# Chosen attention heads: LSTM states summed as they come, weights loaded by head number on the sync queue, TensorE's work in program order

## The chip, the cores and the metric

The kernel runs on one core of a Trainium2 chip (trn2). The core has five engines with a queue of instructions each: PE (matrix multiplication and transposes, results in PSUM banks), DVE (vector operations), ACT (scalar functions, also copies), POOL (general-purpose cores, which here also issue indirect DMAs) and SP (which issues DMAs). The metric is the time of the whole kernel on the device, in microseconds; lower is better.

## What is computed

The reference is a network of two layers on x of shape [8, 512, 256] (8 batch rows, 512 positions, width 256), with a condition vector per row. Layer 0 is a modulated linear map, an attention with graph weights, an LSTM and a mixture of attention heads; layer 1 is an adaptive low-rank map, causal attention, a recurrent layer and a mixture of experts. The change concerns the LSTM's output and what reads it, the mixture of heads:

```python
dist = jax.nn.softmax(jnp.mean(x @ Wr + br, axis=1), axis=-1)   # x: the LSTM's states
top_vals, top_idx = jax.lax.top_k(dist, 4)                      # 4 of 16 heads per row
g = ...                                                         # softmax gate of each chosen head
Qk, Kk, Vk = chosen heads of (x @ W + b), times g               # 64 wide each
attn = softmax(Qk @ Kk.T / 8)                                   # [8, 4, 512, 512]
out = (attn @ Vk).reshape(B, S, 256) @ Wo + bo
```

The mean over positions goes before the product with Wr, so the kernel needs the sum of each LSTM state over the 512 positions. Which four heads a batch row uses is known only once all 512 steps of the LSTM are done.

## The kernel before

**Order of work.** The profiled execution shows: layer 0's modulation and attention up to about 600 us; the LSTM, 512 steps of 2.4 us, up to 1896 us; the chosen heads (`routed_heads`) from 1896 to 2353 us; then layer 1.

**LSTM.** Each step multiplies the last state with the weights on PE (L631), transposes the gates on DVE (L637, L641), applies tanh on ACT (L638, L649) and writes the new state, doubled, into `ring` (DVE, L650), a buffer of eight steps. Each eighth step, POOL copies the eight states, halved, into hT, which holds all states as [128, 2, 8, 512] (L662). Side work is laid into the steps: the next projection of the inputs (`proj`, sums at L601), the rest of the attention (`rest`, in steps 0 to 6 of 16) and the first layer-1 weights (`extra`, in steps 13 to 15 of 16, while it lasts; its sum `ws` is DVE's L988). PE, ACT and DVE follow the order in which this loop is written (`manual_schedule`).

**Choosing the heads** (L687 to L754). SP loads wo, wr, br, and later pmv. DVE sums hT over the positions (hsum, L694), PE multiplies with wr (pl), DVE and ACT compute softmax, the four largest and their numbers, gates gq and gh, and from the head numbers two tables of row offsets: wof for the weights, bof for the biases.

**The loads by head** (`gather`, L758). For each batch row b eight indirect DMAs on POOL fetch w, the weights of four heads (L763; each takes 128 rows of 192 numbers, one row per partition, from the offsets in wof), and four fetch the biases bs (L770). w, bs and the reordered copy wq have two buffers each; bg, the biases times the gates, has three. `prepare` makes wq with four copies on POOL (L784) and bg with two operations on DVE (L789, L790).

**The 32 units.** A unit is a batch row b and a chunk c of 128 positions; `scores`, `transposes` and `average` run as a pipeline of three stages, one unit apart:

- `scores(n)`: PE computes four score tiles pe, one per head, each [128, 512] in a PSUM bank of its own (L822, eight matmuls); DVE takes the maximum nm (L828), ACT the exponential with its sum (L829), DVE the reciprocal rc and the scaling sm (L831, L833).
- `transposes(n - 1)`: for each head, PE transposes four 128x128 blocks into pt (L841; two PSUM banks); DVE copies heads 0 and 2, ACT heads 1 and 3 into eT (L843).
- `average(n - 2)`: PE multiplies eT with v into po (L855, heads 0 and 1, then 2 and 3), ACT scales it into oT (L857).

Per batch row once: `project` (pp on PE L800, qk on ACT L802 and L804; queries in the unit c = 1 of the row before, keys in c = 2), `values` (pv L814, copied on DVE L815; in c = 3), `output` (px L863, added to xT on DVE L864), and once in the stage the constants of layer 1 (ppv, L928, at n = 9). pp, pv, po, px and ppv share two PSUM banks (pool pj). Here no order is written out: a planner in the framework orders every engine's instructions, and they wait for one another by semaphores.

Of the kernel before, what the change touches and what calls it, by code (L numbers as in the profile page):

```python
# [551 lines left out]
def lstm(K, hT, rest, weights, extra):  # L552
# [15 lines left out]
    with ExitStack() as es:  # L568
# [54 lines left out]
        for t in range(S):  # L623
            if t % RB == 0:
                last = ring
                ring = rp.tile([P, RB, 2, B], F32, name="ring", tag="ring")
            for dst, lo, hi in parts(t):
                for k in range(2):
                    hp = h0[:, k, :] if t == 0 else (ring[:, t % RB - 1, k] if t % RB else last[:, RB - 1, k])
                    for j in range(4):  # L630
                        mm(dst[32 * j : 32 * j + B], hp, wh[:, k, j * 256 + lo : j * 256 + hi], start=False, stop=(k == 1))  # L631
            if t + 1 < S:
                if t % XB == XB - 1:
                    xw = nxt
                seed(t + 1, xw, parts(t + 1)[:1])
            G = sp.tile([P, 4, 2, 32], F32, name="G", tag="G")
            nc.vector.transpose(G[:, 0:2].rearrange("p g k b -> p (g k b)"), pgi[t % 2].rearrange("p g n -> p (g n)"))  # L637
            nc.scalar.activation(X[:, 0:2], G[:, 0:2, :, 0:B], AF.Tanh)  # L638
            to = sp.tile([P, 2, B], F32, name="to", tag="to")
            for g, ps, th in ((2, pgg, X[:, 2]), (3, pgo, to)):  # L640
                nc.vector.transpose(G[:, g].rearrange("p k b -> p (k b)"), ps)  # L641
                nc.scalar.activation(th, G[:, g, :, 0:B], AF.Tanh)
            pr = sp.tile([P, 2, 2, B], F32, name="pr", tag="pr")
            STT(pr[:, 1], X[:, 1], 1.0, X[:, 3], ALU.add, ALU.mult)
            STT(pr[:, 0], X[:, 0], 1.0, X[:, 2], ALU.add, ALU.mult)
            X = sp.tile([P, 4, 2, B], F32, name="X", tag="X")
            STT(X[:, 3], pr[:, 1], 0.5, pr[:, 0], ALU.mult, ALU.add)
            th = sp.tile([P, 2, B], F32, name="th", tag="th")
            nc.scalar.activation(th, X[:, 3], AF.Tanh, scale=0.5)  # L649
            STT(ring[:, t % RB], to, 1.0, th, ALU.add, ALU.mult)  # L650
            if t % XB == 7 and t - 7 + XB < S:
                proj = project(t - 7 + XB)
                nxt = next(proj)
            next(proj, None)
            if t % XB < 7:
                next(rest, None)
            if t % XB > 12:
                next(extra, None)
            if t + 1 < S:
                seed(t + 1, xw, parts(t + 1)[1:])  # L660
            if t % RB == RB - 1:
                nc.gpsimd.tensor_scalar(  # L662
                    hT[:, :, :, t - RB + 1 : t + 1], ring.rearrange("p t k b -> p k b t"), 0.5, None, ALU.mult
                )
# [2 lines left out]

def routed_heads(K, hT, T):
# [4 lines left out]
    with ExitStack() as es:  # L677
# [13 lines left out]


        hsum = wp.tile([P, 2, B], F32, name="hsum")
        nc.vector.tensor_reduce(hsum, hT, AX.X, ALU.add)  # L694
        pl = pj.tile([B, NH], F32, name="pl", tag="pj")
        for k in range(2):
            mm(pl, hsum[:, k, :], wr[:, k, :], start=(k == 0), stop=(k == 1))
        lg = wp.tile([B, NH], F32, name="lg")
        nc.vector.scalar_tensor_tensor(lg, pl, 1.0 / S, br, ALU.mult, ALU.add)
        nm = wp.tile([B, 1], F32, name="nm")  # L700
        sm = wp.tile([B, 1], F32, name="sm")
        nc.vector.tensor_reduce(nm, lg, AX.X, ALU.max, negate=True)
# [32 lines left out]
            r = slice(64 * f, 64 * f + 64)  # L735
            nc.vector.tensor_copy(gh[r], g4[r, :, :, :, f])

        pcol = wp.tile([P, 2], F32, name="pcol")
        nc.gpsimd.iota(pcol, [[P, 2]], base=0, channel_multiplier=1, allow_small_or_imprecise_dtypes=True)
        pmod = wp.tile([P, 2], F32, name="pmod")  # L740
        for a in range(4):
            r = slice(32 * a, 32 * a + 32)
            nc.vector.tensor_scalar(pmod[r, 0:1], pcol[r, 0:1], -64.0 * (a // 2), None, ALU.add)
            nc.vector.tensor_scalar(pmod[r, 1:2], pcol[r, 0:1], -32.0 * a, None, ALU.add)
        wof = wp.tile([P, B, 2, NA], I32, name="wof")
        for k in range(2):
            nc.vector.tensor_scalar(wof[:, :, k, :], gb[:, :, 1, :], float(D), pcol[:, k : k + 1], ALU.mult, ALU.add)

        bof = wp.tile([P, B, 4], I32, name="bof")
        nc.vector.tensor_scalar(bof[:, :, 0], gs[:, :, 1], 64.0, pmod[:, 1:2], ALU.mult, ALU.add)  # L750
# [7 lines left out]
        def gather(b):  # L758
            w = gp.tile([P, 2, NA, 192], F32, name="w", tag="w")
            bs = gp.tile([P, 4, 3], F32, name="bs", tag="bs")  # L760
            for k in range(2):
                for s in range(NA):
                    nc.gpsimd.indirect_dma_start(  # L763
                        out=w[:, k, s, :],
                        out_offset=None,
                        in_=inp["moh_w"],
                        in_offset=bass.IndirectOffsetOnAxis(ap=wof[:, b, k, s : s + 1], axis=0),
                    )
            for i in range(4):
                nc.gpsimd.indirect_dma_start(  # L770
                    out=bs[:, i, :],
                    out_offset=None,
                    in_=inp["moh_b"],
                    in_offset=bass.IndirectOffsetOnAxis(ap=bof[:, b, i : i + 1], axis=0),
                )
            W[b] = w, bs

        def prepare(b):

            w, bs = W[b]  # L780
            wr_ = gp.tile([P, 2, 2, 2, P], F32, name="wq", tag="wq")
            for k in range(2):
                for i in range(2):
                    nc.gpsimd.tensor_copy(  # L784
                        wr_[:, k, i].rearrange("p h (s r) -> p h s r", s=NA),
                        w[:, k, :, 64 * i : 64 * i + 64].rearrange("p s (h r) -> p h s r", h=2),
                    )
            bg = gp.tile([P, 4], F32, name="bg", tag="bg", bufs=3)
            nc.vector.tensor_scalar(bg[:, 0:2], bs[:, 0:2, 0], gq[:, b : b + 1], None, ALU.mult)  # L789
            nc.vector.tensor_tensor(bg[:, 2:4], bs[:, 2:4, 2], gh[:, b, 0, :], ALU.mult)  # L790
            W[b] = w, bs, wr_, bg

        def project(b, i):
# [3 lines left out]
            for h in range(2):  # L797
# [4 lines left out]
                    nc.scalar.activation(Q[b][:, i, h, :], pp, AF.Identity, bias=bg[:, h : h + 1], scale=gq[:, b : b + 1])  # L802
                else:
                    nc.scalar.activation(Q[b][:, i, h, :], pp, AF.Identity, bias=bs[:, h, 1:2])  # L804

        def values(b):
            w = W[b][0]
            v = V[b] = qp.tile([P, 4, NA, 64], F32, name="v", tag="v")
            for cc in range(2):
                pv = pj.tile([P, 2, NA, 64], F32, name="pv", tag="pj")  # L810
                for c in range(2):
                    at = (2 * cc + c) * P
                    for k in range(2):
                        mm(pv[:, c], hT[:, k, b, at : at + P], w[:, k, :, 128:192], start=(k == 0), stop=(k == 1))  # L814
                nc.vector.tensor_copy(v[:, 2 * cc : 2 * cc + 2], pv)  # L815

        def scores(b, c):
            pe = [psc.tile([P, S], F32, name="pe", tag="pe") for _ in range(NA)]
# [16 lines left out]
        def transposes(b, c):  # L835
            sm = SM.pop((b, c))
            ET[b, c] = []
            for a in range(NA):
# [3 lines left out]
                t = ep.tile([P, 4, P], F32, name="eT", tag="eT")  # L842
                (nc.scalar.copy if a % 2 else nc.vector.tensor_copy)(t, pt)  # L843
                ET[b, c].append(t)

        def average(b, c):
            eT, bg = ET.pop((b, c)), W[b][3]
# [3 lines left out]
            for pr in range(2):  # L851
                for j in range(4):
                    for f in range(2):
                        a = 2 * pr + f
                        mm(po[64 * f : 64 * f + 64, pr, :], V[b][:, j, a, :], eT[a][:, j, :], start=(j == 0), stop=(j == 3))  # L855
            for pr in range(2):
                nc.scalar.activation(OT[b][:, pr, c * P : (c + 1) * P], po[:, pr, :], AF.Identity, bias=bg[:, 2 + pr : 3 + pr], scale=gh[:, b, 0, pr : pr + 1])  # L857

        def output(b):
            for dc in range(2):  # L860
                px = pj.tile([P, S], F32, name="px", tag="pj")
                for pr in range(2):
                    mm(px, wo[:, pr, dc * P : (dc + 1) * P], OT[b][:, pr, :], start=(pr == 0), stop=(pr == 1))  # L863
                nc.vector.scalar_tensor_tensor(xT[:, dc, b, :], px, K.cols[:, 4 + dc : 5 + dc], xT[:, dc, b, :], ALU.add, ALU.add)  # L864

        gather(0)
        prepare(0)
        gather(1)
        project(0, 0)
        project(0, 1)  # L870
        values(0)
        units = [(b, c) for b in range(B) for c in range(4)]
        for n in range(len(units) + 2):
            if n < len(units):
                b, c = units[n]
                scores(b, c)
                if b + 1 < B:
                    if c == 0:
                        prepare(b + 1)
                    elif c == 3:  # L880
                        values(b + 1)
                    else:
                        project(b + 1, c - 1)
                if c == 3 and b + 2 < B:
                    gather(b + 2)
                if n == 9:
                    T.constants(K, wp, pj.tile([64, D], F32, name="ppv", tag="pj"))
            if 0 < n <= len(units):
                transposes(*units[n - 1])
            if n > 1:  # L890
                b, c = units[n - 2]
                average(b, c)
                if c == 3:
                    output(b)

# [804 lines left out]
def two_layers_kernel(tc, *args):  # L1702
    inp, out = dict(zip(NAMES, args)), args[-1]
    with ExitStack() as es:
        K = State(tc, inp, es)
        with tc.tile_pool(name="wd", bufs=1, space=DRAM) as dp, ExitStack() as eh:
# [5 lines left out]
            def states():  # L1712
                hp = eh.enter_context(tc.tile_pool(name="hT", bufs=1, side="right"))
                lw = el.enter_context(tc.tile_pool(name="l_w", bufs=1, side="right"))
                return hp.tile([P, 2, B, S], F32, name="hT"), lw

            with ExitStack() as e0:
# [143 lines left out]
```

## Time and profile before

| what | us |
|---|---|
| median of three runs | 4411.29 (4408.77 to 4412.3) |
| profiled execution | 4559.43 |
| its span, first to last instruction | 4557.5 |
| chosen heads: whole stage | 1896 to 2353, 457 |
| of these before the first projection on PE (L800) | 32.9 |
| PE busy in the stage | 357.6 |
| DVE, ACT, POOL busy in the stage | 225.9, 174.8, 104.1 |

The profiled execution is 3.4% longer than the median. In it PE is busy for 79% of the span and DVE for 50%; the mean clock granted to PE is 0.901 of full speed. The ends of matmuls are modelled in this profile, and a wait for several semaphores is put down to the one that came last. A row of a timeline gives start, duration, engine, line, operation, output and inputs, count, and in brackets the engine's idle time before it and what ended it. L numbers are lines of the kernel before.

### The profile page before, as it was taken

The numbers are of one execution on the slowest core, as the hardware profiler recorded it, in microseconds if no ns is written. First come the engines' busy times: TensorE is split into PE (matmuls) and PEld (weight loads), VectorE is DVE, ScalarE is ACT, GpSimd is POOL, SyncE is SP. The second block draws the span as 40 slices with busy tenths as digits, with TensorE's granted clock in tenths as the row PEclk, the third lists the DMA queues.
The fourth block names the chain that finished last, engine by engine and source line by source line (L and its number), as shares of the span: only waits on it lengthen the run. The fifth ranks groups of instructions, "written<-read, shape, count | busy, mean of one in ns | idle before, by whom it ended". The sixth has DMA issues, their size and how long they took to land.

```text
span 4557.5 us, 148382 instructions
## 1 busy us (share of the span) xinstructions
PE 3581.0 (79%) x63838; PEld 2335.1 (51%) x63838; DVE 2275.6 (50%) x8665; ACT 1421.0 (31%) x5215; POOL 898.2 (20%) x1534
## 2 busy tenths in 40 slices
PE   7800068888888888578889999999999988989785
PEld 5500045555555555345545555555555545667564
DVE  3300046666666666444547676666667633333332
ACT  2100013333333333234434334343334312323142
POOL 0077700000000000142102222222212211020312
PEclk9955579999999999888999999999999988989698
DMA  2100000000000000200000000000000021343267
GB/s 79 38 1 1 0 17 19 14 19 19 14 4 4 4 4 4 65 25 15 8 2 1 1 1 1 1 1 1 1 1 1 1 96 40 112 124 117 92 209 221
DMA packets 104003, 157.22 MB, mean 34 GB/s; under 512 B 21264, under 2 KB 73776, under 8 KB 102960
## 3 DMA queue, kind: packets, MB, share of 16 engines
q1 hardware_dynamic: 72064, 108.46, 7.9%
q0 software_dynamic: 18432, 23.28, 1.8%
q10 hardware_dynamic: 12848, 15.99, 1.0%
q8 instruction: 500, 8.19, 0.8%
q14 instruction: 159, 1.30, 0.1%
HBM read 107.82 MB, written 41.02 MB: 33 GB/s over the span
## 4 chain that ended last, share of the span: by engine, by line
PE 58%; DVE 20%; another core or an unknown queue 8%; issue 5%; ACT 5%; DMA 2%; POOL 0%; ACTq 0%; SPq 0%; DVEq 0%; POOLq 0%
PE pgi L631 7%; PE pg L1279 5%; PE pe L1113 4%; PE po L1167 3%; PE pt L1152 3%; DVE G L641 3%; PE px L597 3%; PE pp L1080 3%; PE pv L1098 3%; PE px L1183 2%; DVE G L637 2%; PE pg L1501 2%; ACT th L649 2%; PE pe L822 2%
## 5 line engine op out<-in xcount | busy, mean ns | idle before, releaser
L631 PE MATMUL pgi<-wh,ring 128*8 128x128 f32 x8176 | 319.3, 274 | 215.8 <-DVE ring L650 211.8
L1133 ACT ACTIVATE sm<-sm,nm 128x388 f32<-128x388 f32 (+3 forms) x512 | 283.6, 555 | 252.4 <-DVE nm L1129 250.9
L1284 DVE STREAM_TRANSPOSE ring<-h 128x64 f32<-128x64 f32 x512 | 125.6, 245 | 446.0 <-ACT h L1283 429.2
L638 ACT ACTIVATE X<-G 128x32 f32<-128x32 f32 x512 | 117.0, 229 | 686.0 <-DVE G L637 677.5
L631 PEld LDWEIGHTS pgi<-wh,ring 128*8 128x8 f32 x8176 | 177.8, 89 | 280.0 <-DVE ring L650 277.6
L441 PE MATMUL pA<-ohl,ohh 128*32 128x16 f32 x512 | 29.9, 215 | 369.7 <-DVE ohl L438 284.6
L637 DVE STREAM_TRANSPOSE G<-pgi 128x128 f32<-128x128 f32 x512 | 162.1, 317 | 271.4 <-PE pgi L631 271.4
L1279 PE MATMUL pg<-wh,ring 128*8 128x64 f32 x8176 | 229.5, 236 | 80.3 <-DVE ring L1284 67.7
L1080 PE MATMUL pp<-hn,wqkv 128*128 128x512 f32 x512 | 281.0, 689 | 11.0 <-DVE hn L1066 11.0
L420 POOL DMA_INDIRECT gath<-sdr,idx x256 | 253.1, 989 | 99.5 <-issue 77.7
L1283 ACT ACTIVATE h<-pg 128x64 f32<-128x64 f32 x512 | 114.2, 223 | 504.1 <-PE pg L1279 439.3
L1113 PE MATMUL pe<-kt,qt 32*128 32x132 f32 (+3 forms) x2048 | 259.2, 472 | 0.1
L1142 POOL COPY pme<-sm 128x4 f32<-128x4 f32 x512 | 126.4, 247 | 655.1 <-DVE sm L1138 650.6
L1152 PE MATMUL pt<-ident,sm 128*128 128x128 f32 x1280 | 211.1, 287 | 45.8 <-DVE eT L1154 45.6
L1152 PEld LDWEIGHTS pt<-ident,sm 128*128 128x128 f32 x1280 | 151.0, 145 | 166.0 <-DVE eT L1154 77.3
L1279 PEld LDWEIGHTS pg<-wh,ring 128*8 128x8 f32 x8176 | 127.1, 93 | 196.2 <-DVE ring L1284 151.8
L1167 PE MATMUL po<-eT,v 128*64 128x128 f32 x2560 | 206.1, 281 | 17.2 <-DVE rr L1084 15.3
L441 PEld LDWEIGHTS pA<-ohl,ohh 128*32 128x32 f32 x512 | 28.4, 156 | 371.9 <-DVE ohl L438 285.9
L631 PE MATMUL pgo<-wh,ring 128*8 128x64 f32 x8176 | 208.7, 219 | 0.1
L611 PE MATMUL pgi<-xw,ident 128*8 128x128 f32 x4096 | 208.0, 273 | 0.8 <-DVE xw L601 0.5
L631 PE MATMUL pgg<-wh,ring 128*8 128x64 f32 x8176 | 208.5, 219 | 0.0
L1138 DVE TENSOR_SCALAR sm<-sm,rc 128x388 f32<-128x388 f32 (+3 forms) x512 | 199.8, 433 | 5.2
(499 smaller groups left out, 7884.0 us busy)
## 6 DMA issues: line engine op xcount, KB each, us to landing
w<-in_experts_dram SPq DMA_DIRECT2D x124, 384.0 KB
x<-xs SPq DMA_DIRECT2D x124, 128.0 KB
ys<-y SPq DMA_DIRECT2D x124, 128.0 KB
xs<-zero ACTq DMA_DIRECT2D x2, 4736.0 KB
w<-in_ada_w_dram SPq DMA_DIRECT2D x16, 512.0 KB
gath<-sdr,idx POOLq DMA_INDIRECT x256
out_dram<-acc SPq DMA_DIRECT2D x32, 128.0 KB
wqkv<-in_w_qkvT_dram SPq DMA_DIRECT2D x1, 3072.0 KB
```

What stands on the lines that cost most here:

```text
L420: nc.gpsimd.indirect_dma_start(out=gath[:, c : c + 1], out_offset=None, in_=sdr[:, :], in_offset=bass.IndirectOffsetOnAxis(ap=idx[:, c : c ...
L597: mm(px[:, n * 512 : n * 512 + 512], xc[:, k], wx[:, k, n * 512 : n * 512 + 512], start=(k == 0), stop=(k == 1))
L611: mm(dst[32 * j : 32 * j + B], pick[:, t % XB, :], xw[:, j * 256 + lo : j * 256 + hi], start=True, stop=False)
L631: mm(dst[32 * j : 32 * j + B], hp, wh[:, k, j * 256 + lo : j * 256 + hi], start=False, stop=(k == 1))
L637: nc.vector.transpose(G[:, 0:2].rearrange("p g k b -> p (g k b)"), pgi[t % 2].rearrange("p g n -> p (g n)"))
L1080: mm(pp, T.wqkv[:, k, 0 : 2048].rearrange("p (i g h n) -> p i g h n", i=2, g=4, h=2)[:, i, g, h], self.hn[b][:, k, :], start=(k == 0), sto ...
L1113: mm(pe[a][:, 0 : w - lo], q[r, h, at], k[r, h, lo:w], start=(h == 0), stop=(h == 1))
L1133: nc.scalar.activation(sm[a][:, 0:w], sm[a][:, 0:w], AF.Exp, bias=nm[:, a : a + 1], scale=-1.0, accum_out=su[:, a : a + 1])
L1138: nc.vector.tensor_scalar(sm[a][:, 0:w], sm[a][:, 0:w], rc[:, a : a + 1], None, ALU.mult)
L1152: nc.tensor.transpose(pt[:, j, :], sm[a][:, 4 + j * P : 4 + (j + 1) * P], K.ident)
L1167: mm(po[64 * f : 64 * f + 64, pr, :], v[:, j, 64 * a : 64 * a + 64], eT[a][:, j, :], start=(j == 0), stop=(j == c))
L1279: mm(pg[32 * j : 32 * j + B], hp, M.wh[:, k, 64 * j : 64 * j + 64], start=False, stop=(k == 1))
```

## The change

Four edits go together.

1. **Sums within the LSTM.** Each eighth step, after the step's other work, DVE sums `ring` over its eight states into `hpart` (64 such partial sums, [128, 64, 2, 8], 4 KB per partition, in the pool that holds hT). hsum then sums hpart instead of hT; since the ring holds doubled states, the factor is 0.5/S instead of 1/S.
2. **Weights by head number on SP.** wof holds the first row of each chosen head. SP reads it from SBUF into a register (`value_load`) and issues one plain DMA per head (256 rows, 192 KB) with that offset: four register loads and four DMAs per batch row in place of eight indirect DMAs on POOL. The four indirect DMAs of the biases stay on POOL. In the built kernel SP's order is: the loads for b = 0 and 1, then all other 24 register loads, then the other DMAs.
3. **wq of b = 0 on DVE**, the others as before on POOL.
4. **PE in program order.** In the loop over the units PE follows the order in which the code is written. project, values, average, output and constants become generators that yield after each piece (half of a projection, of the values, of the average or of the output); `give` runs one piece of the first that has any left. Per unit PE's order is: scores, first half of average, transposes of head 0 and 1, second half of average, transposes of head 2, a piece of project or values, transposes of head 3, the next piece, then what is left (output, constants). DVE and ACT are still ordered by the planner; outside the LSTM's sums and this stage, all engines have the order of before.

```diff
@@ -659,6 +659,7 @@
             if t + 1 < S:
                 seed(t + 1, xw, parts(t + 1)[1:])
             if t % RB == RB - 1:
+                nc.vector.tensor_reduce(K.hpart[:, t // RB], ring.rearrange("p t k b -> p k b t"), AX.X, ALU.add)
                 nc.gpsimd.tensor_scalar(
                     hT[:, :, :, t - RB + 1 : t + 1], ring.rearrange("p t k b -> p k b t"), 0.5, None, ALU.mult
                 )
@@ -667,6 +668,14 @@
 
 
 
+
+
+def give(queue):
+
+    while queue:
+        if next(queue[0], queue) is not queue:
+            return
+        queue.pop(0)
 
 
 def routed_heads(K, hT, T):
@@ -691,12 +700,12 @@
 
 
         hsum = wp.tile([P, 2, B], F32, name="hsum")
-        nc.vector.tensor_reduce(hsum, hT, AX.X, ALU.add)
+        nc.vector.tensor_reduce(hsum, K.hpart.rearrange("p n k b -> p k b n"), AX.X, ALU.add)
         pl = pj.tile([B, NH], F32, name="pl", tag="pj")
         for k in range(2):
             mm(pl, hsum[:, k, :], wr[:, k, :], start=(k == 0), stop=(k == 1))
         lg = wp.tile([B, NH], F32, name="lg")
-        nc.vector.scalar_tensor_tensor(lg, pl, 1.0 / S, br, ALU.mult, ALU.add)
+        nc.vector.scalar_tensor_tensor(lg, pl, 0.5 / S, br, ALU.mult, ALU.add)
         nm = wp.tile([B, 1], F32, name="nm")
         sm = wp.tile([B, 1], F32, name="sm")
         nc.vector.tensor_reduce(nm, lg, AX.X, ALU.max, negate=True)
@@ -735,16 +744,15 @@
             r = slice(64 * f, 64 * f + 64)
             nc.vector.tensor_copy(gh[r], g4[r, :, :, :, f])
 
-        pcol = wp.tile([P, 2], F32, name="pcol")
-        nc.gpsimd.iota(pcol, [[P, 2]], base=0, channel_multiplier=1, allow_small_or_imprecise_dtypes=True)
+        wof = wp.tile([P, B, NA], I32, name="wof")
+        nc.vector.tensor_scalar(wof, gb[:, :, 1, :], float(D), None, ALU.mult)
+        pcol = wp.tile([P, 1], F32, name="pcol")
+        nc.gpsimd.iota(pcol, [[0, 1]], base=0, channel_multiplier=1, allow_small_or_imprecise_dtypes=True)
         pmod = wp.tile([P, 2], F32, name="pmod")
         for a in range(4):
             r = slice(32 * a, 32 * a + 32)
             nc.vector.tensor_scalar(pmod[r, 0:1], pcol[r, 0:1], -64.0 * (a // 2), None, ALU.add)
             nc.vector.tensor_scalar(pmod[r, 1:2], pcol[r, 0:1], -32.0 * a, None, ALU.add)
-        wof = wp.tile([P, B, 2, NA], I32, name="wof")
-        for k in range(2):
-            nc.vector.tensor_scalar(wof[:, :, k, :], gb[:, :, 1, :], float(D), pcol[:, k : k + 1], ALU.mult, ALU.add)
 
         bof = wp.tile([P, B, 4], I32, name="bof")
         nc.vector.tensor_scalar(bof[:, :, 0], gs[:, :, 1], 64.0, pmod[:, 1:2], ALU.mult, ALU.add)
@@ -758,14 +766,9 @@
         def gather(b):
             w = gp.tile([P, 2, NA, 192], F32, name="w", tag="w")
             bs = gp.tile([P, 4, 3], F32, name="bs", tag="bs")
-            for k in range(2):
-                for s in range(NA):
-                    nc.gpsimd.indirect_dma_start(
-                        out=w[:, k, s, :],
-                        out_offset=None,
-                        in_=inp["moh_w"],
-                        in_offset=bass.IndirectOffsetOnAxis(ap=wof[:, b, k, s : s + 1], axis=0),
-                    )
+            for s in range(NA):
+                row = nc.sync.value_load(wof[0:1, b, s : s + 1], min_val=0, max_val=(NH - 1) * D)
+                nc.sync.dma_start(out=w[:, :, s, :], in_=inp["moh_w"][bass.ds(row, D), :].rearrange("(k p) n -> p k n", p=P))
             for i in range(4):
                 nc.gpsimd.indirect_dma_start(
                     out=bs[:, i, :],
@@ -781,7 +784,7 @@
             wr_ = gp.tile([P, 2, 2, 2, P], F32, name="wq", tag="wq")
             for k in range(2):
                 for i in range(2):
-                    nc.gpsimd.tensor_copy(
+                    (nc.gpsimd if b else nc.vector).tensor_copy(
                         wr_[:, k, i].rearrange("p h (s r) -> p h s r", s=NA),
                         w[:, k, :, 64 * i : 64 * i + 64].rearrange("p s (h r) -> p h s r", h=2),
                     )
@@ -802,6 +805,7 @@
                     nc.scalar.activation(Q[b][:, i, h, :], pp, AF.Identity, bias=bg[:, h : h + 1], scale=gq[:, b : b + 1])
                 else:
                     nc.scalar.activation(Q[b][:, i, h, :], pp, AF.Identity, bias=bs[:, h, 1:2])
+                yield
 
         def values(b):
             w = W[b][0]
@@ -813,6 +817,7 @@
                     for k in range(2):
                         mm(pv[:, c], hT[:, k, b, at : at + P], w[:, k, :, 128:192], start=(k == 0), stop=(k == 1))
                 nc.vector.tensor_copy(v[:, 2 * cc : 2 * cc + 2], pv)
+                yield
 
         def scores(b, c):
             pe = [psc.tile([P, S], F32, name="pe", tag="pe") for _ in range(NA)]
@@ -842,6 +847,7 @@
                 t = ep.tile([P, 4, P], F32, name="eT", tag="eT")
                 (nc.scalar.copy if a % 2 else nc.vector.tensor_copy)(t, pt)
                 ET[b, c].append(t)
+                yield
 
         def average(b, c):
             eT, bg = ET.pop((b, c)), W[b][3]
@@ -853,8 +859,11 @@
                     for f in range(2):
                         a = 2 * pr + f
                         mm(po[64 * f : 64 * f + 64, pr, :], V[b][:, j, a, :], eT[a][:, j, :], start=(j == 0), stop=(j == 3))
+                if pr == 0:
+                    yield
             for pr in range(2):
                 nc.scalar.activation(OT[b][:, pr, c * P : (c + 1) * P], po[:, pr, :], AF.Identity, bias=bg[:, 2 + pr : 3 + pr], scale=gh[:, b, 0, pr : pr + 1])
+            yield
 
         def output(b):
             for dc in range(2):
@@ -862,36 +871,44 @@
                 for pr in range(2):
                     mm(px, wo[:, pr, dc * P : (dc + 1) * P], OT[b][:, pr, :], start=(pr == 0), stop=(pr == 1))
                 nc.vector.scalar_tensor_tensor(xT[:, dc, b, :], px, K.cols[:, 4 + dc : 5 + dc], xT[:, dc, b, :], ALU.add, ALU.add)
+                yield
+
+        def constants():
+            T.constants(K, wp, pj.tile([64, D], F32, name="ppv", tag="pj"))
+            yield
 
         gather(0)
         prepare(0)
         gather(1)
-        project(0, 0)
-        project(0, 1)
-        values(0)
+        for pieces in (project(0, 0), project(0, 1), values(0)):
+            for _ in pieces:
+                pass
         units = [(b, c) for b in range(B) for c in range(4)]
-        for n in range(len(units) + 2):
-            if n < len(units):
-                b, c = units[n]
-                scores(b, c)
-                if b + 1 < B:
-                    if c == 0:
-                        prepare(b + 1)
-                    elif c == 3:
-                        values(b + 1)
-                    else:
-                        project(b + 1, c - 1)
-                if c == 3 and b + 2 < B:
-                    gather(b + 2)
-                if n == 9:
-                    T.constants(K, wp, pj.tile([64, D], F32, name="ppv", tag="pj"))
-            if 0 < n <= len(units):
-                transposes(*units[n - 1])
-            if n > 1:
-                b, c = units[n - 2]
-                average(b, c)
-                if c == 3:
-                    output(b)
+
+
+        with K.tc.manual_schedule(engines={mybir.EngineType.PE}):
+            for n in range(len(units) + 2):
+                more = [average(*units[n - 2])] if n > 1 else []
+                if n < len(units):
+                    b, c = units[n]
+                    scores(b, c)
+                    if b + 1 < B:
+                        if c == 0:
+                            prepare(b + 1)
+                        else:
+                            more.append(values(b + 1) if c == 3 else project(b + 1, c - 1))
+                    if c == 3 and b + 2 < B:
+                        gather(b + 2)
+                    if n == 9:
+                        more.append(constants())
+                if n > 1 and units[n - 2][1] == 3:
+                    more.append(output(units[n - 2][0]))
+                give(more)
+                for a, _ in enumerate(transposes(*units[n - 1]) if 0 < n <= len(units) else ()):
+                    if a:
+                        give(more)
+                while more:
+                    give(more)
 
 
 
@@ -1712,6 +1729,7 @@
             def states():
                 hp = eh.enter_context(tc.tile_pool(name="hT", bufs=1, side="right"))
                 lw = el.enter_context(tc.tile_pool(name="l_w", bufs=1, side="right"))
+                K.hpart = hp.tile([P, S // 8, 2, B], F32, name="hpart")
                 return hp.tile([P, 2, B, S], F32, name="hT"), lw
 
             with ExitStack() as e0:
```

## The prediction

> **What bounds the kernel now.** I read the page's slices first, then the stage's stretches, then the engines' timelines at three places. The page (slices of 113.9 us) shows the routed-heads stage, 1896 to 2353 us, in slices 17 to 21:
>
> ```profile
> PE   7800068888888888578889999999999988989785
> POOL 0077700000000000142102222222212211020312
> PEclk9955579999999999888999999999999988989698
> ```
>
> PE rises to 8 and 9 tenths only from slice 19; before, it waits while POOL works. The stage in stretches (PE, PEld, DVE, ACT, POOL busy, clock, DMA share, GB/s):
>
> ```profile
> 1896.00:1928.50 32.50, 0.95 (x6) 0.67 (x6) 14.94 (x45) 0.60 (x3) 12.26 (x15) 0.50 0.15 41
> 1928.50:1969.00 40.50, 29.75 (x91) 14.77 (x91) 12.59 (x29) 10.74 (x23) 27.39 (x36) 0.73 0.15 40
> 2072.40:2125.00 52.60, 44.49 (x298) 27.38 (x297) 26.37 (x56) 21.64 (x52) 12.85 (x16) 0.90 0.06 16
> 2228.50:2275.40 46.90, 42.17 (x297) 26.05 (x298) 26.10 (x54) 21.75 (x52) 0.00 (x0) 0.96 0.00 1
> ```
>
> The third and fourth rows are the same work for one batch row (four units, one per 128 positions); only the third has indirect DMAs on POOL (12.85 us), and it takes 5.7 us more. The start: the timelines of DVE, POOL and PE.
>
> ```profile
> 1896.82 8.69 DVE L694 TENSOR_REDUCE hsum<-hT 128x16 f32<-128x8192 f32 x1 [0.75 <-POOL hT L662]
> 1913.62 1.03 POOL L763 DMA_INDIRECT w<-in_moh_w_dram,wof  x1 [16.74 <-issue]
> 1928.86 9.44 PE L800 MATMUL pp<-hT,wq 128*128 128x512 f32 x16 [17.89 <-POOL wq L784]
> 1952.45 0.16 DVE L790 TENSOR_TENSOR bg<-bs,gh 128x2 f32<-128x2 f32 x1 [2.20 <-DMA bs<-in_moh_b_dram,bof]
> 1954.07 6.57 PE L822 MATMUL pe<-qk 32*128 32x512 f32 x16 [10.39 <-issue]
> ```
>
> The sum, then twelve indirect DMAs on POOL (1.25 us apart), hold the first projection until 1928.86. DVE then waits for b=2's bias gathers (1952.45) before its first maximum, and PE stands for 10.39 us and returns cold (6.57 us for what takes 2.00 later). In the middle:
>
> ```profile
> 1995.43 0.81 ACT L857 ACTIVATE oT<-po,bg,gh 128x128 f32<-128x128 f32 x2 [5.13 <-PE pt L841]
> 1996.92 1.29 DVE L828 TENSOR_REDUCE nm<-pe 128x1 f32<-128x512 f32 x2 [7.01 <-remote]
> 1994.29 0.94 POOL L763 DMA_INDIRECT w<-in_moh_w_dram,wof  x1 [0.30 <-issue]
> 2302.14 1.09 PE L841 MATMUL pt<-ident,sm 128*128 128x128 f32 x8
> 2306.77 1.09 PE L841 MATMUL pt<-ident,sm 128*128 128x128 f32 x8 [2.08 <-DVE eT L843]
> ```
>
> During the eight w gathers of 1985.54 to 1995.23, PE's groups po and pe, issued by 1991, are reported done only at 1995.4 and 1996.9, just after the last gather; the same happens at 2037, 2092, 2145 and 2197. The last two rows are a quiet unit: two transposes, then PE waits 2.08 us until DVE empties a PSUM bank.
>
> **What the Trainium skill says.** "DMA: Bandwidth & Descriptors", SWDGE vs HWDGE vs iDMA: gathers from GpSimd have their descriptors computed by its cores and written to rings in SBUF, DMAs issued from SP have not, and are immune to what disturbs those rings. The trace has both sides: 1.25 us apart on POOL; on SP elsewhere 7 load-and-issue pairs in 7.30 us. "SBUF — State Buffer", Who interferes with whom: PE shares no port with GpSimd or DMA. The trace disagrees with that as a whole account, for PE is late by some 4 us in each w burst; the mechanism I don't know. "TensorE: Matmul & The Clock Gate", Part 1: half clock after an idle window of about 3.4 us, full after as much work. The trace agrees roughly: 1.00 in 2240 to 2252, with a wait of 1.32 us; 0.88 in the next 12 us, with one of 2.08 us; pe x16 3.17 instead of 2.00 after it.
>
> **The change, part by part** (times of the profiled execution).
>
> *Start.* hsum reads 1024 instead of 8192 elements: 1.2 us by another line's row (L130, 128x1024, 1211 ns) instead of 8.69. That isn't all won: lg needs br, issued at 1897.02, and a small load lands about 1.9 us after its issue (ab, 1.91), so lg moves from 1906.24 to about 1899.5, −6.7, and the offsets are complete at about 1906.7. The w loads of b=0 take 4 x 1.05 on SP and 1.9 to land: 1912. They aren't last. By the built order DVE does the bias products of b=0 and half those of b=1 ahead of b=0's wq copies (now on DVE, some 0.3 us each): six bias gathers at 1.25 from 1906.9, 1.5 us landing: 1915.6, and the first projection at 1916.3 instead of 1928.86, −12.6. Then b=2's bias gathers, which wait for their buffer (ACT qk, about 1927.7): 6.3 us later, 1934, the first maximum, instead of 1952.53. PE pauses some 3 us instead of 10.39; the second score group starts at about 1935.2, and one unit with a projection later (10.3) the third, at 1945.5; in the trace its 14 matmuls run at 1969.00 and two just before, say 1968.9. Start: −23.4. Unknown here: what SP's loads cost (all 24 later register loads stand ahead of b=2's w on SP: 24 x 0.27 us, or at the pair's 1.05 us 25 us, covered until 1939, and b=2's w is needed from about 1975). Ends −18 and −27.
>
> *w loads off POOL.* Heads with gathers last (2228.42 − 2072.35) / 3 = 52.0 us, the one without 46.83: 5.2 us. The bias gathers stay, and in their bursts (2027.55 to 2032.28) oT came about 1.1 us late. So 4.1 x 5 heads = −20.5. Ends: 0, if it is the bytes that disturb PE or if it appears only under the profiler, and −26.
>
> *PE in program order.* Before, the four units of the quiet head take, without clock dips, 14.80 (pp and px), 11.22 (pv), 8.38, 10.12 (pp): 44.5. After, PE per unit: pe 1.93, half of po 1.05, pt 0.5 x 2, half of po 1.05, then the third pt, which needs a bank that DVE's eT copy empties. By the trace that copy is done 2.02 + 4.49 us after pe's start (2300.21, 2302.23, 2306.72); two pt more, 1.0: 7.5 us with 1.4 us of waiting. The pieces come behind the wait and cost their full 3.6 to 3.7: 7.5 + 14.9 + 11.25 + 11.25 = 44.9. That is +0.4 a head, +2.8 in seven: two waits shorter, but nothing laid into them. So I cost the reordering as nearly nothing; ends −8 and +8 (piece sizes, copies).
>
> *Clock.* The quiet head really took 46.83, 2.3 over its 44.5, spent at reduced clock after the 2.08 us waits. After, waits are even, about 1.4 us, near the 1.32 us that left the clock at 1.00. I take half: −1.15 x 8 = −9.2; ends −18 and 0 (the other side is rival C).
>
> *LSTM.* 64 reduces of 128 elements, 286 ns (L1436's 128x128 form lies at this size), directly after the ring's last write. Behind it DVE normally idles 0.75 us until PE's gates: 48 are hidden. 16 share their gap with the adaptive weights' sum, whose wait is then only 0.16 us:
>
> ```profile
> 1891.96 0.32 DVE L637 STREAM_TRANSPOSE G<-pgi 128x128 f32<-128x128 f32 x1 [0.75 <-PE pgi L631]
> 717.58 0.67 DVE L988 TENSOR_TENSOR ws<-pw,b 8x512 f32<-8x512 f32 x1
> 718.41 0.32 DVE L637 STREAM_TRANSPOSE G<-pgi 128x128 f32<-128x128 f32 x1 [0.16 <-PE pgi L631]
> ```
>
> (0.286 − 0.16) x 16 = 2; I take +2.3. Queued behind each are the gates' transposes, for which ACT and then PE wait: without the cover, 64 x 0.286 = +18.3. Lower end 0, since it adds only work to the loop. One wof operation less, the scale 0.5/S, hpart's 4 KB: nothing, inside DVE's wait for bias gathers.
>
> Sum: −23.4 − 20.5 + 2.8 − 9.2 + 2.3 = −48.0. Profiled execution 4559.4 − 48.0 = 4511.4. The median shown, 4411.29, is 0.9675 of the profiled time: 4365.
>
> **Rivals.** *A, everything is won*: no dips (−9.2 more) and bias bursts that cost nothing once the w gathers no longer fill POOL ahead of them (−5.5): −62.7, about 4350. For: they are short, 4 instead of 12 gathers. Against: a 4-burst alone was seen to delay oT. *B, the stall stays*: it comes from the bytes, now at up to 192 KB per 1.05 us on SP, or isn't there without the profiler. Then −27.5: about 4385. For: the skill has no path from POOL to PE. Against: the delays end with POOL's last gather each time, and the clock behind them is 0.5 to 0.6, so PE truly stood. *C, slower*: every unit now has PE waiting at its third transpose for DVE's copy, with all pieces queued behind. If the clock halves after each such wait, the two transposes and the first piece (0.5 + 0.5 + 1.8) take twice as long, 2.8 x 32 units = +89.6; with the rest of the sum (−38.8 without the clock's gain) +50.8: about 4460. It decides from 38.8 / 32 = 1.2 us a unit. For: 1.2 us lost on pe after 2.08 us. Against: 1.00 after 1.32 us. *D, doesn't do what it says*: the stall stays and the reduces are paid in full, −27.5 + 16 = −11.5: about 4400.
>
> **Numbers.** Forecast 0.50, A 0.18, B 0.20, C 0.06, D 0.06. Predicted is the likeliest, 4365. The range leaves out C and A's and D's far tails: 4342 to 4400. Within 0.2% (8.8 us, about what a measurement can tell from no change) falls half of D: same 0.03; slower 0.06; faster 0.91.
>
> **What would show it.** Right: first pp near 1916 and third pe near 1946 (about 2 us later, if the loop pays its reduces); no "remote" wait of 7 us at nm; PE's only regular wait at the third pt, about 1.4 us, clock near 1.00; heads of 45 to 47 us, all alike; DVE's gap before G 0.45 us at every eighth step. Wrong: heads of 50 us with w loads on SP at their slow places (B); pp or pt x4 at double length after each wait (C); LSTM steps of 2.7 us every eighth (D).

## The result and the profile after

The changed kernel takes 4378.23 us (median of 4 runs, 4369.06 to 4380.72), the kernel before, in the runs beside it, 4411.8 us: −33.6 us, ratio 0.9919 with a 95% interval of 0.9906 to 0.9931. It is faster by 0.8%, as forecast; the forecast was 4365, and the time lies inside the stated range of 4342 to 4400.

The profiled execution of the changed kernel took 4380.72 us, in line with the other three. That of the kernel before, from which the prediction worked, took 4559.43 us, and a second profile of the same kernel (the first experiment below) has a span of 4411.1 us. All comparisons from here on use that second profile. The stages, from starts of instructions in the three traces:

| us | before, first profile | before, second profile | after |
|---|---|---|---|
| first LSTM state written, from the start | 641.3 | 572.5 | 571.7 |
| LSTM, first to last state | 1254.6 | 1253.2 | 1253.7 |
| from the last state: router's lg | 10.35 | 10.36 | 3.78 |
| first projection pp on PE | 32.97 | 32.97 | 21.20 |
| first maximum nm | 56.63 | 56.67 | 38.23 |
| first row's output px | 120.9 | 115.7 | 95.3 |
| last matmul of the stage | 456.2 | 427.4 | 390.0 |
| from there to the end | 2205.4 | 2158.0 | 2163.4 |

The stage of the chosen heads is 37.4 us shorter than in the second profile: 20.4 us up to the first row's output, 17.0 us in the seven rows after it. The last row of the table lies between 2158 and 2165 in all traces below, so the 5.4 us there are scatter. The slices of the page of after (109.5 us each; the stage is in slices 17 to 21):

```profile
PE   7901078888888878688889999999999988999885
POOL 0067700000000000111012212222212211130412
PEclk9955599999999999899989999999999988999897
```

The start of the stage in the timelines of DVE, POOL and PE:

```profile
1826.55 1.84 DVE L703 TENSOR_REDUCE hsum<-hpart 128x16 f32<-128x1024 f32 x1
1836.45 1.03 POOL L773 DMA_INDIRECT bs<-in_moh_b_dram,bof  x1 [10.06 <-issue]
1845.93 0.28 DVE L792 TENSOR_SCALAR bg<-bs,gq 128x2 f32<-128x2 f32 x1 [2.79 <-DMA bs<-in_moh_b_dram,bof]
1846.63 8.97 PE L803 MATMUL pp<-hT,wq 128*128 128x512 f32 x16 [12.91 <-DMA w<-in_moh_w_dram]
1863.55 0.16 DVE L793 TENSOR_TENSOR bg<-bs,gh 128x2 f32<-128x2 f32 x1 [2.25 <-DMA bs<-in_moh_b_dram,bof]
1865.18 6.58 PE L827 MATMUL pe<-qk 32*128 32x512 f32 x16 [4.19 <-ACT sm L834]
```

The sum has shrunk from 8.69 to 1.84 us; the first projection follows 0.7 us after the bias product at 1845.93, which waited for the sixth bias gather, as the prediction's walk has it. (The wait of PE is put down to the DMA of w; DVE's copies from w started at 1846.13, behind that product.) The second score group still takes 6.58 us, although PE stood only 4.19 us before it instead of 10. The granted clock in these 6.58 us was 0.50, which would make 4 us of the usual 2.00. The rest is no matter of the clock: the products of the four heads start one after the other, at 1865.18, 1865.85, 1866.51 and 1867.98, each just after ACT's exponential of the group before has read its bank, and so do not run side by side. One unit in the middle, on PE:

```profile
1902.18 2.00 PE L827 MATMUL pe<-qk 32*128 32x512 f32 x16
1904.12 1.09 PE L861 MATMUL po<-eT,v 128*64 128x128 f32 x16
1905.14 1.09 PE L846 MATMUL pt<-ident,sm 128*128 128x128 f32 x8
1906.16 1.09 PE L861 MATMUL po<-eT,v 128*64 128x128 f32 x16
1908.74 1.09 PE L846 MATMUL pt<-ident,sm 128*128 128x128 f32 x8 [1.49 <-DVE eT L848]
1909.77 2.00 PE L827 MATMUL pe<-qk 32*128 32x512 f32 x16
```

That is 7.6 us for a unit without pieces, with one wait of 1.49 us, where the prediction had 7.5 and 1.4.

### The profile page after: what moved, and what is told of

Read it like the earlier page. It is cut to its first block, busy times and chain, and to the rows that moved or that the text cites. A ratio compares the mean times of both kernels' runs of the same rounds, so it can differ in the third digit from the quotient of the medians.

```text
span 4378.9 us, 148586 instructions
## 1 busy us (share of the span) xinstructions
PE 3530.6 (81%) x63838; PEld 2306.3 (53%) x63838; DVE 2289.0 (52%) x8732; ACT 1418.7 (32%) x5215; POOL 826.4 (19%) x1466
## 3 DMA queue, kind: packets, MB, share of 16 engines
q14 instruction: 162, 1.33, 0.1%
## 4 chain that ended last, share of the span: by engine, by line
PE 41%; DVE 9%; ACT 3%; DMA 2%; issue 2%; SPq 0%; ACTq 0%; POOL 0%; DVEq 0%; POOLq 0%
PE pe L1130 5%; PE pg L1296 4%; PE po L1184 3%; PE pt L1169 3%; PE pp L1097 3%; PE pg L1518 3%; PE pv L1115 3%; PE px L1200 3%; DMA x<-xs 2%; DVE sm L1155 2%; PE pe L827 1%; ACT sm L1150 1%; PE pp L803 1%; PE py L1534 1%; PE pg L1280 1%
## 5 line engine op out<-in xcount | busy, mean ns | idle before, releaser
L420 POOL DMA_INDIRECT gath<-sdr,idx x256 | 243.1, 950 | 99.5 <-issue 77.7
L1184 PE MATMUL po<-eT,v 128*64 128x128 f32 x2560 | 206.1, 281 | 17.2 <-DVE rr L1101 15.3
L1146 DVE CUSTOM_DVE_ANT_0 sm<-pe,mask 128x260 f32<-128x260 f32 (+2 forms) x384 | 144.7, 424 | 98.0 <-PE pe L1130 97.3
```

Of the source, the lines that this page charges most:

```text
L420: nc.gpsimd.indirect_dma_start(out=gath[:, c : c + 1], out_offset=None, in_=sdr[:, :], in_offset=bass.IndirectOffsetOnAxis(ap=idx[:, c : c ...
L1146: nc.vector.tensor_tensor_reduce(out=sm[a][:, lo:w], in0=pe[a][:, 0 : w - lo], in1=T.mask[:, S - n + lo : 4 + S], scale=-1.0 / 8.0, scalar ...
L1184: mm(po[64 * f : 64 * f + 64, pr, :], v[:, j, 64 * a : 64 * a + 64], eT[a][:, j, :], start=(j == 0), stop=(j == c))
```

## Experiments

Three theories were to be told apart. T: the 5 us stalls at the weight gathers belong to the one execution that the first profile caught, and the gain consists of the start and of PE's clock, which follows the length of PE's waits. R: the gathers stall PE in every run. R2 and R3, below, deny that the clock follows the waits, and that a wait can be filled with other work. In the end T holds in its direction, but its account of the program order is too simple: the clock is less than half of the busy time that the order saves.

**The kernel before, a second profile** (no edit).

> The kernel before, unchanged, with a second profile. Theory T (the 5 us stalls at the weight gathers belong to the one execution that the first profile caught, and the timed runs do not have them): about 4411 us in the profile too, the heads stage near 424 us instead of 457, no wait of 7 us in front of nm. Rival R (the gathers stall TensorE in every run): the stalls are there again, the stage is 445 us or longer.

Measured: 4412.46 us, ratio 0.9997 (0.9988 to 1.0006), stage 427.4 us. ACT and POOL during a burst of eight weight gathers, in this second profile:

```profile
1919.66 0.59 ACT L843 COPY eT<-pt 128x512 f32<-128x512 f32 x1 [2.85 <-PE pt L841]
1921.06 0.81 ACT L857 ACTIVATE oT<-po,bg,gh 128x128 f32<-128x128 f32 x2 [0.81 <-issue]
1921.03 0.95 POOL L763 DMA_INDIRECT w<-in_moh_w_dram,wof  x1 [0.30 <-issue]
1924.78 0.95 POOL L763 DMA_INDIRECT w<-in_moh_w_dram,wof  x1 [0.31 <-issue]
```

The burst runs from 1916.04 to 1925.72; oT is written in the middle of it, not after it, after a wait of 0.81 us where the first profile had 5.13. The rows of one batch row each, the first with gathers on POOL, the second without:

```profile
2087.10:2132.70 45.60, 40.49 (x297) 25.18 (x296) 26.82 (x55) 21.79 (x52) 13.37 (x16) 1.00 0.07 19
2132.70:2179.50 46.80, 42.08 (x298) 26.06 (x297) 26.20 (x54) 21.78 (x52) 0.00 (x0) 0.96 0.00 1
```

The row with gathers is no longer than the one without. T holds and R falls: 28.8 us of the stage in the first profile, and 69 us before the LSTM and 47 us after the stage, were in that execution alone. What held it up stays open, since no later run shows it.

**Parts alone.** The partial sums only (the LSTM's reduce, hsum and the factor, as in the change's diff):

> Only the partial sums within the LSTM. T and R alike: lg 6.6 us earlier after the last LSTM step; the LSTM's own length unchanged (about 1254 us) if the reduces hide, +2 us if those beside the adaptive weights' sum are paid, +18 us if all are. Total 4405 if hidden, 4407 or 4423 otherwise.

Measured: 4409.53 us, ratio 0.9995 (0.9987 to 1.0003), unclear. In its trace lg comes at 3.78 us, the first projection 6.74 us earlier, the LSTM takes 1252.6 us; but from the first row's output to the end of the stage it takes 315.1 us instead of 311.7, at a clock of 0.96 instead of 0.97. So the start gains its 6.6 us, and the 18 us of the case that every reduce is paid are not there (the LSTM's length differs by up to 5 us among the traces, so 2 us would not show in it). In this one trace 3.4 us go back through the clock; the other two traces with the planner's order have 311.8 us, so this may be scatter.

The weights on SP only, in the planner's order:

```diff
-            for k in range(2):
-                for s in range(NA):
-                    nc.gpsimd.indirect_dma_start(out=w[:, k, s, :], ...)
+            for s in range(NA):
+                row = nc.sync.value_load(wof[0:1, b, s : s + 1], ...)
+                nc.sync.dma_start(out=w[:, :, s, :], in_=inp["moh_w"][bass.ds(row, D), :]...)
```

> Only the weights loaded by head number on SP, wq copies all on POOL, planner's order. T: the start is shorter by some 6 to 13 us (POOL has 4 instead of 12 gathers per row), nothing in the middle: 4398 to 4405. R: the stalls go as well, 20 us more: 4380 to 4385.

Measured: 4404.41 us, ratio 0.9982 (0.9974 to 0.9989). The first projection moves from 32.97 to 28.03 us, the first maximum from 56.67 to 44.99; from the first row's output to the end it takes 311.8 us, as before (311.7). The gathers in the middle cost nothing; only those at the start did.

**All but the program order.**

> The whole change but TensorE's program order (the planner orders TensorE as before). T: the start alone, 4385 to 4390, so that the program order with its even waits of 1.5 us and full clock is worth 7 to 12 us. R: the order is worth nothing, as predicted (+3 us): 4375 to 4378, same as the changed kernel.

Measured: 4396.0 us, ratio 0.9963 (0.995 to 0.9976), −16.5 us: less than T's −21 to −26, since the second score group still takes 6.58 us. The stage is 18.2 us shorter at its last matmul: all of it is won at the start, and the rest takes 311.8 us again. So TensorE's program order is worth 4396.0 − 4378.2 = 17.8 us, about half of the gain: R falls, and T's 7 to 12 us were too few. The stretch from about the first row's output to the last matmul in both kernels (PE, PEld, DVE, ACT, POOL busy, clock, DMA share, GB/s), first of before, second profile:

```profile
1941.40:2253.00 311.60, 276.03 (x2006) 173.35 (x2006) 175.07 (x352) 141.89 (x340) 52.94 (x64) 0.97 0.04 11
```

and of after:

```profile
1920.70:2215.00 294.30, 254.00 (x2008) 158.81 (x2007) 170.99 (x350) 139.64 (x341) 21.64 (x32) 1.00 0.04 12
```

PE does the same 2006 to 2008 matmuls in 22.0 us less, at a clock of 1.00 instead of 0.97, while its idle time has grown from 35.4 to 40.3 us (summed from the timelines; 26 waits for eT, 1.49 us in the median, 1.71 at most). The clock is the smaller part of the 22.0 us. The trace of before has, in this stretch, five pieces of 3.41 us each at a clock of 0.50 and is at 1.00 otherwise; at half speed through 17.1 us PE loses 8.5 us. The other 13.5 us are saved at full clock. One row of after shows it, beside the row of before from 2087.10 above, which was at 1.00 as well and kept PE busy for 40.49 us:

```profile
2102.00:2146.00 44.00, 38.06 (x297) 23.66 (x296) 25.61 (x52) 21.37 (x52) 0.00 (x0) 1.00 0.00 1
```

The same 297 matmuls take 2.4 us less, and it is the order that does it: the run without program order differs from the changed kernel in nothing else, and in its stretch PE is busy for 277.42 us with 20.5 us at half clock, so that 13.2 us of the difference to 254.00 are saved at full clock there too. The planner cuts groups in two. In each row of before it lays px into a score group:

```profile
2131.67 1.12 PE L822 MATMUL pe<-qk 32*128 32x512 f32 x2
2132.72 3.70 PE L863 MATMUL px<-oT,wo 128*128 128x512 f32 x8
2136.35 1.99 PE L822 MATMUL pe<-qk 32*128 32x512 f32 x14
```

Cut up, the group takes 1.12 + 1.99 = 3.11 us instead of the 2.00 of a whole one; and po in parts of 10 and 22 (0.87 + 1.52) or of 6 and 26 takes 2.39 us instead of the 2 x 1.09 of two halves, in nearly every unit. Over the stretch pe and po make up some 12 of the 13.5 us. Before, the waits are also uneven:

```profile
2153.02 0.87 PE L855 MATMUL po<-eT,v 128*64 128x128 f32 x10
2155.21 1.09 PE L841 MATMUL pt<-ident,sm 128*128 128x128 f32 x8 [1.32 <-DVE eT L843]
2156.23 1.52 PE L855 MATMUL po<-eT,v 128*64 128x128 f32 x22
2157.69 2.00 PE L822 MATMUL pe<-qk 32*128 32x512 f32 x16
...
2164.25 1.25 PE L841 MATMUL pt<-ident,sm 128*128 128x128 f32 x8 [2.08 <-DVE eT L843]
2165.43 1.54 PE L855 MATMUL po<-eT,v 128*64 128x128 f32 x10
2166.90 2.74 PE L822 MATMUL pe<-qk 32*128 32x512 f32 x16
```

After the wait of 1.32 us, pe takes its 2.00 us; after that of 2.08 us, 2.74, and po x10 1.54 instead of 0.87. Eight of the waits in the stretch are of 2.08 to 2.36 us, but only five were followed by half the clock. One of the longest was not:

```profile
2119.05 1.09 PE L841 MATMUL pt<-ident,sm 128*128 128x128 f32 x8 [2.35 <-DVE eT L843]
2120.08 0.87 PE L855 MATMUL po<-eT,v 128*64 128x128 f32 x10
2120.88 2.00 PE L822 MATMUL pe<-qk 32*128 32x512 f32 x16
```

The difference lies in where a wait falls. In the traces the clock changes only at the borders of fixed slots of 3.41 us. The wait of 2.08 us lay within one slot (the first row below, busy for 1.33 of 3.41 us; the second row is the next slot, at half clock). That of 2.35 us was cut by the border of two, so that no more than 1.80 us of it fell into a single slot (third row):

```profile
2161.63:2165.04 3.41, 1.33 (x15) 1.09 (x12) 3.06 (x8) 2.17 (x7) 0.00 (x0) 1.00 0.00 0
2165.04:2168.46 3.42, 3.42 (x21) 2.08 (x23) 0.74 (x2) 1.40 (x3) 0.00 (x0) 0.50 0.02 5
2117.26:2120.67 3.41, 1.61 (x17) 1.45 (x18) 3.38 (x8) 1.69 (x4) 1.76 (x4) 1.00 0.11 29
```

In this stretch of all nine traces from the second profile on, every drop from 1.00 to 0.50 comes right after a slot in which PE stood for 1.94 us or more, and none after one with 1.84 us or less.

**Longer waits on purpose.** Whether the waits cause the clock was tested by making them longer with the same work:

```diff
                 for a, _ in enumerate(transposes(...)):
-                    if a:
+                    if a > 1:
                         give(more)
```

> The changed kernel with the second half of the average moved behind the third transpose, so that TensorE's wait in every unit grows from 1.49 to about 2.5 us; the work is the same. Theory T (waits of 2 us and more cost clock, waits of 1.5 us do not, and that is what program order gained): 31 x 1.03 = 32 us for the wait itself, and the clock of the stage falls from 1.00 to 0.97 or less, 20 us more: about 4430. Rival R2 (the gain has another cause, the clock does not follow the waits): 4410, clock still 1.00.

Measured: 4461.6 us, ratio 1.0112 (1.0097 to 1.0128), slower than both. The same stretch of the stage, and one unit:

```profile
1928.60:2294.00 365.40, 298.59 (x2008) 189.82 (x2007) 173.06 (x350) 142.33 (x341) 21.79 (x32) 0.87 0.04 10
```

```profile
2054.03 0.66 PE L846 MATMUL pt<-ident,sm 128*128 128x128 f32 x4 [2.51 <-DVE eT L848]
2054.62 1.96 PE L861 MATMUL po<-eT,v 128*64 128x128 f32 x16
2056.51 1.12 PE L846 MATMUL pt<-ident,sm 128*128 128x128 f32 x4
```

The waits cost 26.5 us more of idle time (66.8 instead of 40.3), and the clock, 0.87, another 44.6 us of busy time: po x16 takes 1.96 us instead of 1.09 and pt x4 1.12 instead of 0.60. Another 9.0 us are lost before the first row's output. T's direction holds, with twice the clock loss it named; R2 falls. Waits of 1.5 us in every unit leave the clock at 1.00, waits of 2.5 us in every unit do not. What T adds in brackets, that this is what the program order gained, holds for 8.5 of the 22.0 us of busy time alone.

**The wait filled.**

```diff
                     if a:
                         give(more)
+                    if a == 1:
+                        give(more)
```

> The changed kernel with a piece of the next row's projection laid into the wait for the third transpose's bank (two pieces of work given after the second transpose instead of one). T: in the 22 units that have a piece the wait of 1.49 us goes: 30 us less, 4348, waits left only in the units without a piece. R3 (the two banks of the pool of pieces hold a piece up as long as the copy holds the transpose): no gain, 4378.

Measured: 4354.88 us, ratio 0.9871 (0.9856 to 0.9886), 23.3 us less than the changed kernel. A unit with a projection, on PE:

```profile
2044.91 2.00 PE L827 MATMUL pe<-qk 32*128 32x512 f32 x16
2046.84 1.09 PE L861 MATMUL po<-eT,v 128*64 128x128 f32 x16
2047.87 1.09 PE L846 MATMUL pt<-ident,sm 128*128 128x128 f32 x8
2048.89 1.09 PE L861 MATMUL po<-eT,v 128*64 128x128 f32 x16
2049.91 1.98 PE L803 MATMUL pp<-hT,wq 128*128 128x512 f32 x4
2051.74 0.60 PE L846 MATMUL pt<-ident,sm 128*128 128x128 f32 x4
2052.47 1.98 PE L803 MATMUL pp<-hT,wq 128*128 128x512 f32 x4
2054.29 0.60 PE L846 MATMUL pt<-ident,sm 128*128 128x128 f32 x4
2054.82 2.00 PE L827 MATMUL pe<-qk 32*128 32x512 f32 x16
```

9.9 us instead of 11.0, without a wait; idle time in the stretch falls from 40.3 to 15.3 us. R3 falls. T's 30 us are not reached: PE stands 25 us less, but is busy 5.7 us longer.

**Three bias buffers** (`bufs=3` on bs), so that the third row's bias gathers don't wait for ScalarE:

> The changed kernel with three bias buffers instead of two, so that the bias gathers of the third row do not wait for ScalarE. T: the first maximum moves from 38.2 to about 36 us after the last LSTM step, TensorE's pause before the second score group shrinks by 2.6 us and that group (6.58 us, cold) gets part of its 4.6 us back: 3 to 7 us less, 4371 to 4375. Rival: the weights bind next, no gain.

Measured: 4372.82 us, ratio 0.9912 (0.9899 to 0.9926). The first maximum comes at 35.60 instead of 38.23 us, and the last matmul at 386.5 instead of 390.0; against the changed kernel the two intervals overlap, so the 5.4 us of the medians aren't shown by the times alone. The trace has 3.6 us, the lower part of T's range, but not T's whole reason: the pause does shrink, and the group behind it gets nothing back.

```profile
1861.72 6.58 PE L827 MATMUL pe<-qk 32*128 32x512 f32 x16 [1.57 <-ACT sm L834]
```

Here half the clock (from 1863.20) follows a wait of only 1.57 us, so the 1.94 us found above are no bound for other work: in this group the heads' products come one after the other. Why it drops here is not shown.

**All together**, with the output product of a row laid three units later, where there is no other piece:

> Both, and the output product of a row moved three units later, into the units that have no other piece. T: waits gone in nearly all 30 units, about 40 us less, and the start's 3 to 7: 4331 to 4336. R3: as the changed kernel, 4372 to 4378.

Measured: 4343.79 us, ratio 0.9847 (0.9833 to 0.986): the fastest version, 34.4 us below the changed kernel. In the middle of its stage PE is busy for 96% of the time:

```profile
1940.30:2184.00 243.70, 235.15 (x1804) 145.21 (x1800) 154.70 (x319) 125.22 (x308) 14.48 (x24) 1.00 0.04 11
```

T's 4331 to 4336 was 8 us too low. It took all of the idle time away; from 60 us after the last LSTM state to the end of the stage PE stands 13.0 us (48.2 in the changed kernel), and it is busy 2.6 us longer.

## Why the prediction was right, and where its sum was not

The side and the range were right, and in part by luck. The sum, −46 us for a measured −33.6, comes out near because one term of it, −20.5, was empty, and the program order, put at next to nothing, brought 8.6 us.

- **Start, −23.4.** The mechanism and each step of it hold: lg moves by 6.58 us (predicted 6.7), the first projection by 11.8 (12.6), the first maximum by 18.4 (18.5). The size fails at the last step: the second score group was to run warm after a pause of some 3 us; it took 6.58 us again, at half the clock and with its heads one after the other. So the third came 17.1 us earlier by its first two matmuls and 19.2 by the other 14, not 23.4. (The prediction put the first two of before at "just before" 1969.00; they ran at 1966.90.) At the first row's output the start is worth 20.4 us, without the program order 18.3.
- **w loads off POOL, −20.5.** This step failed. Its stalls are in the first profile only; the second has none, and with the loads on SP the middle of the stage takes 311.8 instead of 311.7 us. Rival B named this ("isn't there without the profiler"), except that the later profiles don't have it either. The profiled execution stood 148 us above the median, and the prediction spread that evenly with the factor 0.9675; in truth the excess lay in three places, 69 us before the LSTM, 28.8 in the stage and 47 after it. With the Trainium skill ("SBUF — State Buffer", Who interferes with whom: PE shares no port with GpSimd or DMA), which the prediction took the first trace to contradict, the second trace agrees.
- **Program order, +2.8, and clock, −9.2.** Together −6.4, measured −17.0. The mis-sized term is the order. The walk of the changed row was near: 44.0 to 44.6 us with waits of 1.5 us (predicted 44.9 and 1.4). But the row before was put at 44.5 us "without clock dips"; the one row of the second profile at full clock takes 45.60, so the order saves 1 us and more a row where it was to cost 0.4: 13.5 us less busy time, as whole groups replace cut ones, against 4.9 us more idle time, −8.6. The clock comes out near its number by luck: half of a loss of 18.4 us was to go; the second profile has a loss of 8.5 us in the seven rows, and all of it went. Rival C, that waiting in every unit costs clock, did not come true at 1.49 us; at 2.5 us it does.
- **LSTM, +2.3.** Nothing, 0.4 us at most: in the 16 steps where the reduce shares its gap with the adaptive weights' sum the step takes 2.520 instead of 2.494 us, and the other 47 steps with a reduce are no longer than before (2.549 and 2.565). A reduce takes 370 ns in the median and not 286, but the transpose behind it starts while it ends:

```profile
647.98 0.67 DVE L1005 TENSOR_TENSOR ws<-pw,b 8x512 f32<-8x512 f32 x1
648.59 0.35 DVE L662 TENSOR_REDUCE hpart<-ring 128x16 f32<-128x128 f32 x1
648.86 0.29 DVE L637 STREAM_TRANSPOSE G<-pgi 128x128 f32<-128x128 f32 x1
```

The new sum, from the traces: −20.4 (start) − 17.0 (order −8.6, clock −8.5) + 0 (w loads in the middle) + 0 (LSTM) = −37.4 in the stage, against −33.6 in the medians, whose interval (0.9906 to 0.9931) allows −30 to −41.

## What to carry to other kernels

Before a profile is read for its stalls, its execution's time is to be held against the timed runs; if it stands some per cent above them, the excess has places, and a stall that ends for no visible reason ("remote") is the first suspect. When the busy time of the engine that limits a stage falls, look for the reason in two places: the clock it was granted, and the order of its work. Here 8.5 of 22.0 us were clock, and 13.5 us came from groups of matmuls that were no longer cut in two. Where that engine waits in every unit, the size of the single wait matters more than the sum: 40 us in even waits of 1.5 us left the clock at 1.00, and 35 us with waits of up to 2.4 us among them did not. Laying side work into these waits, and not behind them, was worth another 23.3 us.

## What the runs showed of the hardware

- TensorE's granted clock over the same stretch was 1.00 with a wait of about 1.5 us in every unit of 7.6 to 14.5 us, 0.97 with waits of up to 2.4 us in some, 0.87 with about 2.5 us in every unit. It fell from 1.00 to 0.50 after slots of 3.41 us with at least 1.94 us of standing, and not after 1.84 us (nine traces, this stretch alone; at the start of the stage a wait of 1.57 us was followed by 0.50 too). That is less than the idle window of about 3.4 us which the prediction cites and took the trace to bear out roughly. The Trainium skill, "TensorE: Matmul & The Clock Gate", Why this matters for your kernels, advises against idle gaps of more than about 3 us; here gaps of 2.1 us already cost, when they fell into one slot.
- Score matmuls of four heads, 32 rows each: 16 of them took 2.00 us in one group, and 1.12 + 1.99 us when cut into 2 and 14.
- A register load from SBUF and the DMA issued with it took 1.17 us a pair on SP (eight pairs from 1836.63 to 1844.85), the load itself 0.27 us.
- A sum over elements 64 bytes apart took longer for each element: hsum reads 1024 elements per partition in 1836 ns after the change, 1.8 ns each, and 8192 that lie side by side in 8.69 us before it, 1.1 ns each. No run changes the step alone.
